# A new order of operations for each batch of a cross-attention kernel on one NeuronCore

## The chip, the core and the metric

The kernel runs on one core of a Trainium2 chip. The metric is the device time of one execution in microseconds (us): the median over several runs. A core has engines that work beside each other, each through its own instructions in order: TensorE (PE in the profile; its weight loads are listed as PEld), VectorE (DVE), ScalarE (ACT), GpSimd (POOL), and SyncE (SP), which here only issues transfers. They wait for one another at semaphores. Matmul results go to PSUM, which this kernel uses as eight banks of 512 float32 for each of 128 partitions.

## The reference

32 independent batches; `x` and `y` (in the inputs `ctx_2048`) have 256 channels by 1024 columns, float32.

```python
x_q = jnp.einsum('oc,bcn->bno', w_qk, y)
x_k = jnp.einsum('oc,bcn->bon', w_qk, x)
x_v = jnp.einsum('oc,bcn->bon', w_v, x) + b_v[None, :, None]
energy = jnp.einsum('bnc,bcm->bnm', x_q, x_k)
attention = jax.nn.softmax(energy, axis=-1)
attention = attention / (1e-07 + attention.sum(axis=1, keepdims=True))
x_r = jnp.einsum('bcn,bnm->bcm', x_v, attention)
x_r = jax.nn.relu(jnp.einsum('oc,bcn->bon', w_t, x - x_r) + b_t[None, :, None])
return x + x_r
```

Per batch there are keys from x, a 1024 by 1024 energy matrix, a softmax along its rows, a second division by its column sums, the values weighted by it, a last projection, a relu and the addition of x.

## The kernel before

**Forms.** Every operand of a matmul is kept twice: a HIGH form, the value rounded to fp32r, and a LOW form, the rest. A *product* of two 128-row operands is three matmuls, in the order of `ORDER` (line 46): high by high, high by low, low by high (left by right). So a right operand's HIGH form is read by the first and the third matmul of a product, a left operand's HIGH form by the first and the second. HIGH forms are mostly written by ACT, LOW forms by POOL or DVE, and most of them have one buffer that every batch uses again: `gf` (keys), `xf` (x), `yd` and `ysum` (y), `uf` (values).

**Chains of seven.** The keys (`k`), the projection of x (`x`) and the four pairs of energy tiles (`E0` to `E3`) are 2 by 2 block products that are made with seven products instead of eight. `chain` (line 385) names them P1 to P7. P1, P6 and P7 add to one bank, "a". Between them ACT copies that bank out (`r1`, `r2`, `r3`, into the ring `rs`), since P6 adds to what P1 left and r1 must have been read first. P2 goes to bank "b", P5 and then P3 to bank "c", P4 to bank "d" (in `k` and `x` to "a"). DVE makes the four blocks from the banks and the copies (`c11`, `c22`, `c12`, `c21`); P3 can add to bank "c" only after `c22` has read it. For a chain of keys the banks a, b, c are 2, 0, 1; of x 6, 4, 5; of energy a, b, c, d are 3, 0, 1, 2.

**Softmax.** A pair of chains E0 to E3 leaves two tiles of 128 by 1024: the even tile (n = 2p) in banks 0 and 1, the odd one (n = 2p + 1) in banks 2 and 3. For tile n: `exp` on ACT (with the row sums), `ri` (reciprocal, DVE), then for each half h `h` (HIGH form of the softmax weights in the ring `efs`, ACT), `l` (LOW form, DVE) and `sum` (their column sums in `acc`, DVE). The next pair's P1 writes bank 3, so it comes after `h`, `l` and `sum` of the odd tile's half 1; in the same way E3's tile 7 must be read out of bank 2 before kP1, and tile 6 out of bank 1 before kP5. `A` + n, c, h is the product that adds tile n's share to the output rows c, half h, in banks 4 to 7.

**Rest of a batch.** `V` + q, half: values, 12 matmuls of 256 columns each, to banks 4 to 7 before the x chain uses them; `vh`, `vl` their forms. `kc`, `kT`, `khD`, `klD`, `kTh`, `kTl`, `kh21`, `kl21`: blocks and sums of the keys and their forms in `gf`. `xh`, `xl`, `xT`, `xTh`, `xTl`: forms and sums of x in `xf`; `xTh1` is ACT's copy of the second pair of sums into the HIGH form that xP6 and xP4 read. `yh`, `yl`, `ys`, `ysh`, `ysl`: the same of y. `cols`, `inv`, `turn`: column sums, their reciprocals, and these turned (DVE). `div`, `join`, `pos`, `add`, `st`: division (DVE), addition of the projection (POOL), relu (ACT), addition of x by a transfer that POOL issues, and the store.

**What sets the order.** Each such name is a *word*: a small function that issues its instructions. Three tables of words, written out in the kernel, are the whole order: FIRST (batch 0), STEADY (run for batches 1 to 29) and LAST (the last two batches). `do` goes through a table, word by word; a plus ahead of a word means the next batch, a minus the one before. A pair (word, batch) that was done is passed over. `InOrder` (line 51) makes each engine issue in exactly the order of the words, so an instruction that waits holds up all that stands behind it on its engine, while the other engines go on. Waits between engines follow from the data: a word waits for what it reads and for the last readers of what it overwrites. All instructions pass through one helper line, L62 of the profile, so tiles tell them apart: on PE `efs,uf` is an A product, `xf,gws` the key chain, `xf,tws` the x chain, `vws,xf` the values, `gf,yd` the products 1, 2, 4 of an energy chain and `gf,ysum` its products 3, 5, 6, 7.

Of the kernel before, what the change touches and what calls it, by code (L numbers as in the profile page):

```python
# [17 lines left out]
def kernel(  # L18
# [739 lines left out]


    FIRST = """  # L760
        ys01 Sgram Scorner Swt Stp Swtc Sgh0 Ssq Sgh1 Fxh0 Sbvw Fxl0 Sgl Th22 xh1 Fxl1
        yh01 FHH0 Sgraw Sth Svh Fyh FHL0 Svl FHH1 Gh12 FLH0 FLH1 FHL1 yh00 Fraw11 ldy1
        Fkh12 Fraw22 Fkh22 Fkh11 V11 V10 ys02 yl01 ys04 ys03 ysh0 kT1 Fkl11 yl00 Fkl22 kT2
        kh21 Tl22 Fkl12 vh1 yh11 Fyl V00 Stl kT4 Sbias Th12 Gh22 kl21 FE11 kT3 vl1 FE10
        kTh0 Gl12 ysl0 Fmin1 V01 FE00 vh0 kTl0 exp1 FE01 ys11 vl0 ri1 h11 kTh1 ys12 FX11
        kTl1 Gs1 FX01 Fmin0 exp0 yh10 sum11 Gs2 l11 ri0 E1P1 Gl22 sum10 FX00 h00 h01 E1r1
        h10 E1P6 FX10 Fxw0 E1r2 sum00 ys13 ys14 l00 sum01 E1P7 l01 ysh1 l10 E1P5 yl10 E1r3
        E1c22 yl11 E1P4 +ldx0 E1c21 E1P2 Gs3 Gs4 ysl1 E1P3 A101 Fxw1 +xh0 E1c11 exp3 A110
        A001 A100 ri3 h31 E1c12 sum31 A000 l31 GhS exp2 ri2 sum21 h30 E2P1 l30 sum30 E2r1
        h21 +ldx1 A010 E2P6 sum20 E2r2 l21 E2P4 h20 +xT1 E2P7 l20 E2r3 +xT3 Ts3 E2P5 Ts1  # L770
        +xTh0 GlS +xh1 +xl0 E2c22 E2c21 E2P2 A300 exp5 E2c11 ri5 +xT2 A111 E2P3 h51 E2c12
        A310 A011 sum51 l51 h50 A301 exp4 +ldy0 Ts2 A311 E3P1 ri4 A200 sum41 sum50 Ts4
        +xl1 E3r1 +xT4 +xTl0 +ys01 +ys02 sum40 h41 +ldy1 E3P6 l41 A201 +yh01 E3r2 h40 E3P7
        E3r3 l50 l40 E3P5 +xTh1 E3c22 E3P4 E3P2 A210 E3c21 +yh00 ThS E3P3 A510 exp7 +ys04
        +xTl1 E3c11 ri7 E3c12 h70 A211 exp6 l70 sum70 A511 +ys11 +ys13 Tl12 +ys12 A501
        +ys03 ri6 +kP1 sum71 h61 l61 +kr1 A410 +kP6 sum60 +ysh0 +yl00 +yl01 +kr2 A500 +kP7
        sum61 cols +kP5 h60 +kr3 h71 l60 TlS +ys14 +kc22 +kP2 +kP3 +kc11 +kc12 +ysl0 A411
        +kP4 ++ldx0 A400 +kT1 l71 +kT3 +khD +kT2 +kT4 inv +kTh0 +kTh1 turn A711 A401 A710
        +yh10 A610 +klD +kTl1 +kh21
    """  # L780
    STEADY = """
        E0P1 E0r1 yh11 ysh1 -A700 -A701 -A611 E0P6 -div1 kTl0 -A601 kl21 -A600 E0r2 E0P7
        E0P5 -div0 E0r3 E0P4 E0c22 ysl1 yl10 E0P2 E0c21 E0c11 exp1 E0P3 yl11 +xT1 -join1
        -join0 V10 V11 ri1 h11 E0c12 V00 h10 l11 sum11 exp0 l10 ri0 sum10 vh1 E1P1 V01
        sum01 E1r1 h00 vl1 h01 vh0 +ldx1 l01 sum00 E1P6 vl0 l00 E1r2 E1P4 xP1 E1P7 +xh0
        E1r3 E1P5 E1c22 xP2 E1P2 E1c21 xr1 -pos0 E1P3 xP6 A111 xP5 exp3 E1c11 xr2 +xT2
        +xT3 +xT4 xc11 ri3 E1c12 h31 A011 xP7 A100 sum31 l31 exp2 +xl0 ri2 xr3 E2P1 sum30
        h21 h30 E2r1 sum20 A000 xP4 +xTh1 l21 E2P6 xc22 E2r2 h20 sum21 xP3 l30 E2P7 E2P5
        E2P4 xc12 l20 E2r3 E2c22 xw21 +xh1 E2c21 A101 E2P2 A110 E2P3 exp5 E2c11 ri5 E2c12
        h51 exp4 +ldy0 h50 l51 A001 sum51 A010 ri4 +xTl1 A311 A310 +ys01 h41 E3P1 A300  # L790
        E3r1 l41 sum41 E3P6 +xl1 h40 E3P5 E3r2 E3P7 +yh00 +xTh0 sum50 l50 sum40 l40 +ldy1
        E3r3 A200 E3P4 E3P2 A210 -pos1 A301 E3c22 E3c21 exp7 E3c11 ri7 h70 E3P3 A510 +yh01
        A500 A211 E3c12 +ys11 +ys03 -add1 +xTl0 +ys02 +ys04 +ys12 exp6 +yh10 A201 sum70
        l70 ri6 h61 +kP1 A410 sum71 +yl01 +ys13 +ys14 +kr1 h60 sum61 l61 +kP6 +kP5 l60
        sum60 +kr2 +kP7 +kr3 A710 +ysh0 +kP2 +kc22 h71 +kc11 +kP3 +kc12 -st1 A610 +kP4
        -add0 +yl00 +kT1 +ysl0 +kT2 +kT3 l71 +khD ++ldx0 -st0 +kT4 +kTh0 +klD +kTh1 cols
        A511 A400 +kh21 inv turn +kTl1 A501 A411 A401 A711
    """
    LAST = """
        -E0P1 -yh11 -ysh1 -kTl0 --A611 --A700 --A701 -E0r1 -E0P6 --div1 -kl21 --A601 -E0r2  # L800
        --A600 -E0P7 -E0P5 --div0 -E0r3 -E0P4 -E0c22 -E0P2 -E0P3 -E0c21 -exp1 -E0c11 -ysl1
        -ri1 -E0c12 --join1 -h11 -yl10 -yl11 -sum10 -exp0 -V11 -V10 -vh1 -l11 -sum11 -ri0
        -V00 -sum00 -h01 -E1P1 -E1r1 -V01 -vl1 -E1P6 -h00 -h10 -xP1 -l01 -sum01 -E1P5 -l00
        -l10 -vh0 -E1r2 -E1P7 --join0 -E1r3 ldx1 -vl0 -E1P4 -E1P2 -E1c22 -E1c21 -E1c11
        -xr1 xh0 -xP5 -xP2 -xP6 -E1P3 -exp3 -xc11 -A111 -ri3 xT1 -E1c12 -xr2 xT3 xT2 -h31
        -l31 -sum31 -h30 xT4 -xP7 -xr3 -xc22 -A100 -A011 -E2P1 -exp2 -E2r1 -xP3 -ri2 -l30
        -E2P6 -sum30 -xc12 -xP4 -h21 -h20 -E2r2 -E2P4 -sum21 -l21 -E2P7 xh1 -xw21 -E2P5
        xl1 -A311 -A101 -l20 -sum20 -E2r3 -E2c22 -E2P2 -E2c21 xTh0 xTh1 -exp5 -E2c11 -ri5
        -A110 -E2P3 xl0 -A001 -A000 -A010 -A301 -h51 -h50 ldy1 -E2c12 ldy0 xTl0 -l51
        -sum51 -exp4 -E3P1 -ri4 -h41 -E3r1 -A300 -E3P6 -l50 -sum41 -h40 -l41 -E3r2 yh01  # L810
        -sum50 -l40 -sum40 -E3P5 --pos0 -E3P7 -A200 -E3r3 -E3c22 -E3P2 xTl1 ys01 ys11 ys02
        --add0 --pos1 -E3P4 -A310 -A201 -E3P3 -E3c21 -A501 -A211 yh11 -exp7 -E3c11 -A500
        -A210 -ri7 -E3c12 -h70 -l70 -sum70 kP1 yh10 -exp6 -ri6 -sum71 ys12 ys14 ys13 yl10
        ys04 yl01 -h61 kr1 -A510 -h60 -l61 -sum61 kP6 -sum60 kr2 -l60 kP5 kP7 -cols -h71
        yh00 kr3 kc22 --add1 ys03 yl11 -A511 kP2 kc11 -l71 -A401 kP3 kP4 kc12 -A411 ysh0
        -A400 -A410 yl00 -A711 kh21 ysl0 kT1 khD kT2 -inv Zx1 --st1 kT4 kl21 kT3 -A710 klD
        -turn -A611 -A701 ysh1 kTh1 E0P1 -A610 -A700 E0P2 kTl1 kTh0 E0r1 -div1 E0P6 E0r2
        --st0 -A601 -A600 Zx0 kTl0 E0P7 -div0 -join0 E0r3 E0P5 E0c22 E0P4 E0c21 V00 -join1
        E0c11 exp1 E0P3 ri1 E0c12 h11 V10 V11 h10 sum11 l11 exp0 vh1 l10 sum10 E1P1 ri0
        vl1 E1r1 h00 V01 E1P6 h01 l00 E1P4 sum01 xP1 vh0 sum00 l01 E1r2 ysl1 E1P7 E1r3 xr1  # L820
        E1P5 E1P2 vl0 E1c22 -pos1 A111 E1c21 E1P3 E1c11 xP6 exp3 xr2 E1c12 xP2 ri3 h31
        A011 xc11 exp2 xP7 xr3 l31 sum31 A100 ri2 xP5 sum21 E2P1 xc22 sum30 h20 l20 E2r1
        xP4 h21 l21 E2P6 E2r2 xP3 h30 E2P7 xc12 E2P5 l30 A101 E2r3 sum20 E2c22 xw21 E2P4
        E2P2 E2c21 E2c11 E2P3 A110 exp5 A311 A001 ri5 h51 E2c12 A010 A000 exp4 l51 sum51
        E3P1 ri4 A310 h40 E3r1 h41 E3P6 sum50 l40 sum40 E3r2 h50 l41 A300 sum41 l50 E3P7
        E3P5 Zs1 E3P4 E3r3 -pos0 Zs0 E3P2 E3c22 -add1 E3c21 E3P3 exp7 A210 E3c11 E3c12
        A200 -add0 ri7 sum71 A301 A510 A211 h70 exp6 A500 A410 A201 l70 sum70 ri6 A710
        A400 sum60 sum61 A501 h71 Zn1 A511 h60 Zn0 h61 A401 l71 -st1 cols l60 inv A701
        A411 A610 l61 turn A601 Zd10 A700 -st0 A711 Zd01 Zm10 A600 Zm01 A611 Zd00 Zd11
        Za10 Zm00 Za01 Zm11 Zt10 Zt01 Za11 Za00 Zt11 Zt00  # L830
# [47 lines left out]
```

## Time and profile before

| | |
|---|---|
| median of 3 runs | 1894.0 us (1893.49 to 1894.99) |
| the profiled execution | 1892.67 us |
| its span, first to last instruction | 1890.5 us |
| granted TensorE clock, mean | 0.999 |
| PE idle before matmuls of energy, named ACT's `rs` | 9.2 us in 29 waits |
| DVE, ACT, POOL busy | 85%, 76%, 74% of the span |
| HBM | 71 GB/s over the span |

Times within a batch are counted from the span's start. The batch that is looked at closely is batch 10, from 540.75 us, where its E0P1 starts, to 599.22, where the next batch's does. A timeline row has start, busy time, engine, line, operation with output and inputs, and how many equal ones follow each other; in brackets stands the idle time just ahead of it, with the engine and tile that ended it.

### The profile page before, as it was taken

Reading aid. Unit: us, or ns where it says so; the run is one execution under the profiler, and the core shown is the slowest. Engines: PE = TensorE matmul, PEld = TensorE weight load, DVE = VectorE, ACT = ScalarE, POOL = GpSimd, SP = SyncE. Lnnn points to the kernel's source line nnn. Section 1 sums busy time; section 2 is a strip of 40 time slices with the busy share of each in tenths; the row PEclk is TensorE's granted clock in tenths of the full one; section 3 lists DMA queues with packets and bytes.
Section 4 is the critical chain, followed back from the end, with each engine's and each line's share of the span. In section 5 each row is a group of like instructions: output and inputs, shape, how many; then the busy total and the mean of one; then the engine's idle time right before and its main releaser. Section 6 shows DMA issues by size and latency. Waiting matters only on the chain. (4 is left out here: it accounts for less than half of the span.)

```text
span 1890.5 us, 25202 instructions
## 1 busy us (share of the span) xinstructions
PE 1869.4 (99%) x8680; PEld 1499.5 (79%) x8680; DVE 1609.0 (85%) x3044; ACT 1432.2 (76%) x2223; POOL 1400.0 (74%) x975
## 2 busy tenths in 40 slices
...
GB/s 96 36 81 87 45 68 87 80 79 50 74 78 79 79 56 67 79 79 78 64 60 78 79 79 77 49 76 79 83 84 45 72 85 79 79 56 68 68 90 67
DMA packets 46720, 136.76 MB, mean 72 GB/s; under 512 B 4480, under 2 KB 5376, under 8 KB 46592
## 3 DMA queue, kind: packets, MB, share of 16 engines
...
## 5 line engine op out<-in xcount | busy, mean ns | idle before, releaser
L62 PE MATMUL banks<-efs,uf 128*128 128x512 f32 x3072 | 784.3, 390 | 0.0
L62 PEld LDWEIGHTS banks<-efs,uf 128*128 128x128 f32 x3072 | 576.6, 188 | 122.8 <-DVE efs L62 0.3
L62 PE MATMUL banks<-gf,ysum 128*128 128x512 f32 x1524 | 423.2, 400 | 9.2 <-ACT rs L62 9.2
L62 ACT COPY rs<-banks 128x512 f32<-128x512 f32 (+1 forms) x475 | 279.3, 588 | 199.6 <-PE banks L62 199.1
L62 DVE SCALAR_TENSOR_TENSOR efs<-banks,small,efs 128x512 fp32r<-128x512 f32 x512 | 377.9, 744 | 40.6 <-ACT efs L62 37.0
L62 ACT ACTIVATE efs<-banks,small 128x512 fp32r<-128x512 f32 x512 | 339.4, 689 | 34.8 <-DVE small L62 22.3
L62 ACT ACTIVATE banks<-banks,small 128x1024 f32<-128x1024 f32 x256 | 278.8, 1089 | 111.9 <-DVE small L62 107.6
L62 PEld LDWEIGHTS banks<-gf,ysum 128*128 128x128 f32 x1524 | 271.0, 188 | 109.3 <-ACT rs L62 55.2
L62 DVE SCALAR_TENSOR_TENSOR acc<-banks,small,acc 128x512 f32<-128x512 f32 x448 | 329.8, 742 | 21.7 <-ACT efs L62 20.2
L62 PE MATMUL banks<-gf,yd 128*128 128x512 f32 x1158 | 319.1, 392 | 0.4 <-DVE efs L62 0.2
L62 POOL TENSOR_TENSOR xf<-sums,xf 128x1024 fp32r<-128x1024 f32 x62 | 157.6, 2543 | 189.4 <-PE banks L62 116.7
L62 POOL TENSOR_TENSOR sums<-raws 128x256 f32<-128x256 f32 (+1 forms) x188 | 173.6, 931 | 112.3 <-DMA raws<-in_ctx_dram 112.3
L62 PEld LDWEIGHTS banks<-gf,yd 128*128 128x128 f32 x1158 | 212.4, 188 | 49.9 <-POOL gf L62 5.1
L62 POOL TENSOR_TENSOR gf<-sums,gf 128x1024 fp32r<-128x1024 f32 x95 | 226.1, 2408 | 0.6 <-ACT gf L62 0.6
L62 DVE CUSTOM_DVE_ANT_0 banks<-banks,rs,small 128x512 f32<-128x512 f32 x254 | 192.7, 759 | 27.9 <-PE banks L62 11.0
L62 DVE CUSTOM_DVE_ANT_0 banks<-banks,rs 128x512 f32<-128x512 f32 x254 | 180.8, 712 | 37.7 <-PE banks L62 30.6
L62 PEld LDWEIGHTS banks<-vws,xf 128*128 128x128 f32 x1536 | 192.8, 191 | 5.4
L62 PE MATMUL banks<-vws,xf 128*128 128x256 f32 x1536 | 194.3, 283 | 0.0
L62 PE MATMUL banks<-xf,gws 128*128 128x512 f32 x651 | 189.5, 412 | 3.0 <-DVE small L62 0.2
L62 PE MATMUL banks<-xf,tws 128*128 128x512 f32 x651 | 183.0, 390 | 0.0
L62 POOL TENSOR_TENSOR ysum<-sums,ysum 128x1024 fp32r<-128x1024 f32 x64 | 154.4, 2412 | 22.2 <-ACT ysum L62 22.2
L62 POOL TENSOR_TENSOR xf<-raws,xf 128x1024 fp32r<-128x1024 f32 x62 | 149.6, 2414 | 25.5 <-ACT xf L62 25.4
...
## 6 DMA issues: line engine op xcount, KB each, us to landing
...
```

The lines of the kernel that those rows point to most:

```text
L62: self.last = getattr(self.engine, name)(*args, **kwargs)
```

## The change

Only the three tables are different. Every word is there as often as before, in another order, in FIRST, STEADY and LAST. In making the new order the HIGH form of an operand was counted as being read until the third matmul of a product. Of the difference a few lines of STEADY:

```diff
     STEADY = """
-        E0P1 E0r1 yh11 ysh1 -A700 -A701 -A611 E0P6 -div1 kTl0 -A601 kl21 -A600 E0r2 E0P7
...
+        E0P1 -A611 -turn kTh1 kh21 E0r1 kTh0 kl21 -A610 kTl1 -A700 kTl0 E0P6 E0r2 yh11
...
```

The places of which the prediction speaks follow as they stand in the built program. First PE in the second pair's chain: the rows from E2P1 to the A product behind E2P4, of a batch in the middle of the program, before.

```order
L62 MATMUL banks<-gf,yd 128x512 x3
L62 MATMUL banks<-efs,uf 128x512 x3
L62 MATMUL banks<-xf,tws 128x512 x3
L62 MATMUL banks<-gf,ysum 128x512 x3
L62 MATMUL banks<-xf,tws 128x512 x3
L62 MATMUL banks<-gf,ysum 128x512 x6
L62 MATMUL banks<-gf,yd 128x512 x3
L62 MATMUL banks<-efs,uf 128x512 x3
```

They are E2P1, A000, xP4, E2P6, xP3, then E2P7 with E2P5, E2P4 and A101. The same place on PE in the change:

```order
L62 MATMUL banks<-gf,yd 128x512 x3
L62 MATMUL banks<-xf,tws 128x512 x6
L62 MATMUL banks<-gf,ysum 128x512 x3
L62 MATMUL banks<-efs,uf 128x512 x3
L62 MATMUL banks<-gf,ysum 128x512 x6
L62 MATMUL banks<-gf,yd 128x512 x3
L62 MATMUL banks<-efs,uf 128x512 x3
```

These are E2P1, xP4 with xP3, E2P6, A311, then E2P5 with E2P7, E2P4 and A000: the last two products of the x chain are both ahead of E2P6, and two products instead of one stand between E2P6 and E2P7.

ACT beside it, from h21 to xw21: the copies into `rs` are the readings E2r1, E2r2 and E2r3, and the CAST into `xf` from `sums` is xTh1. Before:

```order
L62 ACTIVATE efs<-banks,small 128x512 x2
L62 COPY rs<-banks 128x512
L62 CAST xf<-sums 128x1024
L62 COPY rs<-banks 128x512
L62 ACTIVATE efs<-banks,small 128x512
L62 COPY rs<-banks 128x512
L62 ACTIVATE xe<-banks,xbias 128x512
```

In the change, on ACT, from the same h21, where the two ACTIVATE into `efs` are h30 and h20 and the CAST from `raws` is xh1:

```order
L62 ACTIVATE efs<-banks,small 128x512
L62 COPY rs<-banks 128x512
L62 ACTIVATE efs<-banks,small 128x512 x2
L62 COPY rs<-banks 128x512
L62 CAST xf<-raws 128x1024
L62 COPY rs<-banks 128x512
L62 ACTIVATE xe<-banks,xbias 128x512
```

xTh1 has gone from between E2r1 and E2r2 (it now stands behind E3r2), and xh1 has come between E2r2 and E2r3.

Last, PE from E3P1 into the next batch's keys, before:

```order
L62 MATMUL banks<-gf,yd 128x512 x3
L62 MATMUL banks<-efs,uf 128x512 x3
L62 MATMUL banks<-gf,ysum 128x512 x9
L62 MATMUL banks<-efs,uf 128x512 x3
L62 MATMUL banks<-gf,yd 128x512 x6
L62 MATMUL banks<-efs,uf 128x512 x6
L62 MATMUL banks<-gf,ysum 128x512 x3
L62 MATMUL banks<-efs,uf 128x512 x12
L62 MATMUL banks<-xf,gws 128x512 x3
L62 MATMUL banks<-efs,uf 128x512 x3
L62 MATMUL banks<-xf,gws 128x512 x9
L62 MATMUL banks<-efs,uf 128x512 x3
```

That is E3P1, A300, E3P6 with E3P5 and E3P7, A200, E3P4 with E3P2, A210 with A301, E3P3, four A products, kP1, A410, kP6 with kP5 and kP7, and A710. The same stretch of PE in the change:

```order
L62 MATMUL banks<-gf,yd 128x512 x3
L62 MATMUL banks<-efs,uf 128x512 x6
L62 MATMUL banks<-gf,ysum 128x512 x9
L62 MATMUL banks<-gf,yd 128x512 x3
L62 MATMUL banks<-efs,uf 128x512 x6
L62 MATMUL banks<-gf,yd 128x512 x3
L62 MATMUL banks<-gf,ysum 128x512 x3
L62 MATMUL banks<-efs,uf 128x512 x12
L62 MATMUL banks<-xf,gws 128x512 x3
L62 MATMUL banks<-efs,uf 128x512 x6
L62 MATMUL banks<-xf,gws 128x512 x12
L62 MATMUL banks<-efs,uf 128x512 x3
```

Now E3P1 is followed by A310 and A301 ahead of E3P6, and kP1 by A510 and A501 ahead of kP6; kP6, kP5, kP7 and kP2 follow each other, with A401 ahead of kP3. From E3P7 to kP1 there are nine products (before, ten).

The order of the other words of a batch, with its neighbours, is changed in the same way; the x rows of the batch after next are loaded as `ldx1` at a batch's end and `ldx0` in its second pair, where before it was the other way round. In FIRST, PE's FHH0 and FHL0 (first keys) stand ahead of Ssq (the product of two weight matrices) instead of behind it.

More of the change, by code (lines that the diff above doesn't have):

```diff
@@ L760 @@
     FIRST = """
[L761 to L778, printed above, removed]
@@ new lines @@
+        FX11 E1P6 h01 Gs1 yl10 h00 E1r2 FX00 kTl0 E1P7 +ldx0 l00 l01 l10 Fxw1 sum00 E1r3
+        E1P5 E1P4 +xh0 E1c22 Gs2 E1c21 E1P2 Fxw0 E1P3 A100 Gl12 Gs4 Ts1 yl11 exp3 E1c11
+        Gs3 Ts3 ri3 E1c12 h31 ysl1 Ts2 exp2 A110 l31 sum31 A101 +ldx1 A010 A111 +xl0 GhS
+        ri2 E2P1 h21 A001 E2r1 sum30 sum21 l21 h20 E2P6 +xT3 Ts4 +xT1 l20 +ldy0 E2P5 E2r2
+        h30 sum20 l30 E2P7 E2P2 E2P4 E2r3 A011 +xh1 E2c22 E2P3 +xT2 A301 GlS A000 A201
+        A300 E2c21 A311 E2c11 exp5 ri5 E2c12 h51 l51 sum51 exp4 +yh01 ri4 E3P1 sum50 h41
@@ new lines @@
+        E3r1 h40 +xT4 h50 A211 E3P6 E3r2 l41 sum41 l40 l50 E3P5 E3P7 +xTh1 E3r3 E3P4 sum40
+        E3P2 A310 E3c22 E3c21 E3P3 +xTh0 +xl1 +ys01 +ys02 +yl01 A210 +ys04 +xTl1 exp7
+        +yh00 E3c11 A511 ri7 +ldy1 E3c12 h70 exp6 l70 sum70 ri6 A510 A200 A501 ThS h61
+        +kP1 sum71 A410 l61 +kr1 sum61 +kP6 +xTl0 h60 +ys03 +kr2 +ysh0 TlS +kP5 sum60 +kP7
+        A401 l60 +kP2 +ys11 +kr3 +yl00 cols +kc22 +kP3 A411 A500 +kc11 +kc12 +ys12 h71
+        +ysl0 +kP4 +ys14 A400 +khD +yh10 +kT1 +ys13 l71 +kT2 A701 +klD +kT4 inv +kT3 A710
@@ L787 @@
[L787 to L797, printed above, removed]
+        E0P1 -A611 -turn kTh1 kh21 E0r1 kTh0 kl21 -A610 kTl1 -A700 kTl0 E0P6 E0r2 yh11
```

89 lines of the change are left out of this document (53 added, 36 removed).

## The prediction

> **What bounds the kernel now.** I read the page's first part, then the weight loads' waits, then one batch on TensorE row by row.
>
> ```profile
> span 1890.5 us, 25202 instructions
> PE 1869.4 (99%) x8680; PEld 1499.5 (79%) x8680; DVE 1609.0 (85%) x3044; ACT 1432.2 (76%) x2223; POOL 1400.0 (74%) x975
> ```
>
> TensorE (PE) is named busy for 99%, yet a matmul's shown time overlaps the next one's, so a short stall hides in it. Starts are what count. This is PE's timeline in batch 10; columns are start, busy time, operation with its tiles, count, and idle time before.
>
> ```profile
> 545.52 1.55 PE L62 MATMUL banks<-gf,ysum 128*128 128x512 f32 x6
> ...
> 548.97 4.48 PE L62 MATMUL banks<-vws,xf 128*128 128x256 f32 x36
> 553.28 0.86 PE L62 MATMUL banks<-gf,yd 128*128 128x512 f32 x3
> ...
> 567.10 0.85 PE L62 MATMUL banks<-gf,ysum 128*128 128x512 f32 x3
> 567.79 0.84 PE L62 MATMUL banks<-xf,tws 128*128 128x512 f32 x3
> 568.94 1.65 PE L62 MATMUL banks<-gf,ysum 128*128 128x512 f32 x6 [0.31 <-ACT rs L62]
> 570.43 0.84 PE L62 MATMUL banks<-gf,yd 128*128 128x512 f32 x3
> ...
> 573.83 2.88 PE L62 MATMUL banks<-efs,uf 128*128 128x512 f32 x12
> 576.55 0.84 PE L62 MATMUL banks<-gf,yd 128*128 128x512 f32 x3
> 577.23 0.84 PE L62 MATMUL banks<-efs,uf 128*128 128x512 f32 x3
> 578.07 2.60 PE L62 MATMUL banks<-gf,ysum 128*128 128x512 f32 x9
> 580.51 0.85 PE L62 MATMUL banks<-efs,uf 128*128 128x512 f32 x3
> ```
>
> Twelve wide matmuls start in 576.55 - 573.83 = 2.72 us, 0.227 each, so a product of three is 0.68; a narrow one is (553.28 - 548.97) / 36 = 0.120. A batch has six chains of 7 products and 32 A products, 74 x 3 = 222 wide matmuls, and 4 x 12 = 48 narrow ones; they need 222 x 0.227 + 48 x 0.120 = 56.2 us. The next rows are a whole batch by windows (window, length, busy time of PE and of the weight loads, and so on) and the waits of the weight loads over the span (us, times, longest).
>
> ```profile
> 540.75:599.22 58.47, 58.08 (x272) 46.63 (x270) 50.13 (x95) 44.67 (x69) 43.81 (x32) 1.00 0.27 72
> ...
> PEld banks L62 <- ACT rs L62: 76.4, 191, 1.0
> PEld banks L62 <- DVE sums L62: 15.7, 30, 0.5
> PEld banks L62 <- DVE efs L62: 10.8, 33, 0.4
> ```
>
> A batch takes 58.47 us (540.75 is E0P1's start, 599.22 the next one's), so 2.3 us are stalls. No other engine is over 50.13. The loads of the same batch say where:
>
> ```profile
> 568.94 1.23 PEld L62 LDWEIGHTS banks<-gf,ysum 128*128 128x128 f32 x6 [0.73 <-ACT rs L62]
> ...
> 578.07 1.23 PEld L62 LDWEIGHTS banks<-gf,ysum 128*128 128x128 f32 x6 [0.42 <-ACT rs L62]
> 579.71 0.53 PEld L62 LDWEIGHTS banks<-gf,ysum 128*128 128x128 f32 x3 [0.41 <-ACT rs L62]
> ...
> 588.84 0.53 PEld L62 LDWEIGHTS banks<-xf,gws 128*128 128x128 f32 x3 [0.42 <-ACT rs L62]
> 589.71 0.53 PEld L62 LDWEIGHTS banks<-xf,gws 128*128 128x128 f32 x3 [0.33 <-DVE efs L62]
> 590.50 0.53 PEld L62 LDWEIGHTS banks<-xf,gws 128*128 128x128 f32 x3 [0.26 <-ACT rs L62]
> ...
> 592.93 0.54 PEld L62 LDWEIGHTS banks<-xf,gws 128*128 128x128 f32 x3 [0.52 <-DVE sums L62]
> ```
>
> In order they are E2P7, E3P6, E3P7, kP6, kP5, kP7 and kP3. A load runs ahead of its matmul, so a wait costs less than it shows: at E2P7 nine matmuls from 567.79 took 2.64 instead of 2.04 us, 0.60 lost for a wait of 0.73; from 577.23 twelve took 3.28 instead of 2.72, 0.56 for 0.42 + 0.41. I take wait minus 0.15: 0.58, 0.27, 0.26, 0.27, 0.18, 0.11, 0.37, together **2.04 us a batch**. That is what an order can win.
>
> **Why they wait.** Bank a is written by a product, read by ACT, and added to by the next product.
>
> ```profile
> 567.35 1.05 ACT L62 CAST xf<-sums 128x1024 fp32r<-128x1024 f32 x1 [0.46 <-PE banks L62]
> ...
> 568.31 0.57 ACT L62 COPY rs<-banks 128x512 f32<-128x512 f32 x1
> ...
> 577.43 0.59 ACT L62 COPY rs<-banks 128x512 f32<-128x512 f32 x1 [0.18 <-PE banks L62]
> ```
>
> E3P1 starts at 576.55, its reading at 577.43 (0.88 later), E3P6 at 578.07: 1.52 us from product to product with a free ACT. One product between covers 2 x 0.68 = 1.36, and 0.16 plus a slow second matmul is lost; two between cover 2.04, with 0.52 to spare. E2P7 is worse: ACT stands first in xTh1 (567.35), which waits 0.46 us for xP4, the last reader of the high form that it overwrites; E2r2 starts only at 568.31, where E2P6 at 567.10 would have let it start at 567.98.
>
> **The change, part by part.** No instruction is added or removed; all terms are stalls per batch, and the new table runs for 29 batches.
>
> *E2P7.* Two products now stand between E2P6 and E2P7 (A311 and E2P5), and on ACT xTh1 is gone from before E2r2; behind E2r2 is xh1, whose readers xP2 and xP3 are ahead of E2P6. E2r2 follows h30 and h20, which need nothing from E2P6. Gone: **0.58**, at worst 0.27 stays if these two run late.
>
> *E3P6 and kP6.* Each has two products before it (A310 and A301; A510 and A501). Ahead of E3r1 ACT now has exp4, yh00 and h41; they use the spare 0.52 at the worst. Gone: 0.27 + 0.27 = **0.54**.
>
> *kP5* waits for l61, the last reader of its bank. On DVE l61 gets sum60 ahead of it (0.66 us, the step from 574.72 to 575.38 in the DVE rows below), and on PE kP5 gets one product more ahead of it (0.68) but loses kP6's stall as cover. Gone: **0.10**, between nothing and 0.18.
>
> *Kept.* E3P6 to E3P7 and kP6 to kP7 still have one product between: 0.26 stays, and kP7, which hid behind kP5's wait, rises from 0.11 to 0.26: **-0.15**. kP7 to kP3 still has two: 0.37 stays.
>
> *New waits.* From a pair's last bank-a product to the next pair's first, the chain runs through reading, blocks with minima, exponential, reciprocal and weights. In E2 before (ACT and DVE of the timeline):
>
> ```profile
> 569.94 0.59 ACT L62 COPY rs<-banks 128x512 f32<-128x512 f32 x1 [0.46 <-PE banks L62]
> ...
> 570.74 0.70 DVE L62 CUSTOM_DVE_ANT_0 banks<-banks,rs 128x512 f32<-128x512 f32 x1 [0.48 <-PE banks L62]
> ...
> 571.64 0.76 DVE L62 CUSTOM_DVE_ANT_0 banks<-banks,rs,small 128x512 f32<-128x512 f32 x1
> ...
> 572.50 1.09 ACT L62 ACTIVATE banks<-banks,small 128x1024 f32<-128x1024 f32 x1 [0.44 <-DVE small L62]
> ...
> 573.74 0.16 DVE L62 RECIPROCAL small<-small 128x1 f32<-128x1 f32 x1 [0.31 <-ACT banks L62]
> ...
> 574.03 0.76 DVE L62 CUSTOM_DVE_ANT_0 banks<-banks,rs,small 128x512 f32<-128x512 f32 x1
> ...
> 574.72 0.75 DVE L62 SCALAR_TENSOR_TENSOR efs<-banks,small,efs 128x512 fp32r<-128x512 f32 x1
> 575.38 0.74 DVE L62 SCALAR_TENSOR_TENSOR acc<-banks,small,acc 128x512 f32<-128x512 f32 x1
> ```
>
> E2P7 starts at 568.94, the last reader of E3P1's bank ends at 576.12: 7.18 us, and E3P1 came at 576.55, 0.43 later. In the new order nine products stand between E2P7 and E3P1 and nine between E3P7 and kP1: 10 x 0.68 = 6.8 us. The chain's steps hold some 0.35 us in which it waited for PE itself: 0.12 at the first reading (1.00 against the 0.88 above), and, at the first block, for E2P5, which now is ahead of E2P7:
>
> ```profile
> 580.81 0.58 ACT L62 COPY rs<-banks 128x512 f32<-128x512 f32 x1
> ...
> 581.43 0.70 DVE L62 CUSTOM_DVE_ANT_0 banks<-banks,rs 128x512 f32<-128x512 f32 x1
> ```
>
> That is E3's first block, 0.62 after its reading against 0.80. Another 0.05 is the second block, which waited for E2P4. So the chain needs between 6.83 and 7.18 us for 6.8: E3P1 and kP1 wait between nothing and 0.38 each, and up to 0.1 more in the second matmul. The rows show most of those waits ended by PE, so I lean to the lower end: 0.2 each, **-0.40**. For E1P1 the cover is four products and 36 narrow matmuls, 4 x 0.68 + 36 x 0.120 = 7.04, and for E2P1 eleven products, 7.5: nothing, at worst 0.1.
>
> A wide matmul's pitch of 0.227 sets these covers. The Trainium skill, page "TensorE: Matmul & The Clock Gate", section "Back-to-back issue gap", gives about 216 ns for 512 columns. By it ten products would cover 6.5 us instead of 6.8 and each new wait would be 0.3 us longer, an estimate from that page of 0.6 us a batch less won, about 1891; this trace does not agree, and its 0.227 decides.
>
> *First and last batches.* The first batch's FHH0 and FHL0 now stand before Ssq, where PE idled:
>
> ```profile
> 7.06 1.99 PE L62 MATMUL banks<-z 128*128 128x256 f32 x8 [0.57 <-ACT z L62]
> ```
>
> That is 0.57 us. The rest of FIRST and LAST I cost at nothing, as both have chains with one and with two products between in both versions; the bound is one batch's 2.04 us either way.
>
> **The sum.** 0.58 + 0.54 + 0.10 - 0.15 - 0.40 = 0.67 us a batch; 29 x 0.67 = 19.4, with 0.57 about 20 us. The profiled execution took 1892.7 (span 1890.5), so this gives 1872.7 for it; the median of the runs is 1894.0, 1.3 more: **1874 us**.
>
> **Rivals.** *More is won.* If no new wait appears, 29 x 1.07 + 0.6 = 32 us: 1862; with kP7 as small as now and kP5's wait wholly gone 29 x 1.30 + 0.6 = 38: 1856. For it: the stretches of the chain that waited for PE. Against: 6.83 leaves nothing spare in 6.8.
>
> *The softmax chain becomes the bound (the other side).* Place: from E0P7, E2P7 and E3P7 to the next pair's first product. If the chain needs 7.2 us in the new order too, E1P1 waits 0.16, E3P1 and kP1 0.4 each, with 0.1 for each second matmul 1.2 in all: the 1.07 won is gone, about 1896. From there each tenth costs 0.3 us a batch. If it needs what lay between those products before, 568.94 to 576.55 and, for E0P7 to E1P1, 545.52 to 553.28 (7.76), the waits are 0.7 + 0.3 + 0.95 + 0.95 and 0.4 for second matmuls, 3.3 against 1.07: 29 x 2.2 = 64 us more, 1958. For it: E2's 7.18 is a measured need. Against: in these rows the softmax weights were ready 0.4 us before the product came.
>
> *The waits move to POOL.* klD must end before E0P1's second matmul.
>
> ```profile
> 596.86 4.79 POOL L62 TENSOR_TENSOR gf<-sums,gf 128x1024 fp32r<-128x1024 f32 x2
> ```
>
> The first of these two is klD, ending near 599.26, for a matmul at 599.22 + 0.23: 0.2 to spare. In the new order kT2 and klD still end POOL's queue of the batch. Each tenth more than those 0.2 costs 2.9 us; with half a microsecond late E0P1 waits 0.3 29 x 0.3 = 9 us: 1883, inside the range.
>
> *The change does not do what it says*, that is, ACT still waits for high forms being read: then E2P7's 0.58 stays, 29 x 0.58 = 17 us: 1891.
>
> **Chances.** My forecast (1864 to 1884) 0.55; more won (1855 to 1864) 0.13; the chain, POOL or ACT gives back part, 1884 to 1890, 0.13; all of it, 1890 to 1898, 0.10; slower 0.09, most of it the chain. A measurement of this kernel tells about 0.2% (3.8 us) from no change. Faster 0.81, same 0.10, slower 0.09. Low end: 38 us won, 1856. High end: both new waits at 0.48 and E1P1's at 0.1 leave 1.07 - 1.06, nothing, and the first batch's 0.6: 1893; the range is 1856 to 1893.
>
> **What would show it.** Right: E0P1 to E0P1 falls to about 57.8 us; E2P6, E3P1 and kP1 are each followed about 2.04 us later by the next product of their chain on bank a; the loads' waits on ACT's rs fall from 76.4 to below 40 us; waits at E3P7, kP7 and kP3 stay. Wrong: waits of over 0.6 us at E3P1 or kP1 on DVE, at xP3 on DVE's xe, or at E0P1 on POOL's gf; or a first batch that is later by several microseconds.

## The result, and the profile after

| | before | after |
|---|---|---|
| median | 1893.74 us (1893.36 to 1894.99) | 1876.94 us (1876.58 to 1877.14) |
| the profiled execution | 1892.67 us | 1876.58 us |
| its span | 1890.5 us | 1874.5 us |
| granted TensorE clock | 0.999 | 0.999 |

The changed kernel takes 0.991 of the time before (95% interval 0.9893 to 0.9927): 16.8 us less, where 20 were forecast.

The page's first part of the changed kernel shows nothing of it; busy shares hardly moved.

```profile
span 1874.5 us, 25084 instructions
PE 1861.9 (99%) x8680; PEld 1506.3 (80%) x8680; DVE 1596.7 (85%) x3044; ACT 1439.3 (77%) x2223; POOL 1407.3 (75%) x975
```

Starts show it. These are the rows of PE's timeline with E0P1 of batch 1 and of batch 30, the ends of the 29 batches that STEADY orders; first the kernel before, then the change (start, busy time, operation).

```profile
72.45 1.24 PE L62 MATMUL banks<-gf,yd 128*128 128x512 f32 x3
...
1768.86 0.86 PE L62 MATMUL banks<-gf,yd 128*128 128x512 f32 x3
```

```profile
71.89 0.85 PE L62 MATMUL banks<-gf,yd 128*128 128x512 f32 x3
...
1754.40 0.84 PE L62 MATMUL banks<-gf,yd 128*128 128x512 f32 x3
```

The 29 batches took 1696.41 us and now 1682.51: 13.9 less, 0.48 a batch. (The batches are numbered from 0 here and in the experiments; the "tenth batch" of the rows is batch 9, which stands in the kernel before from E0P1's row at 540.68 to the next one's at 599.17.) The first batch is 72.45 - 71.89 = 0.56 shorter. The last part is (1890.5 - 1768.86) - (1874.5 - 1754.40) = 1.54 shorter. Together 16.0, the whole difference of the spans.

Where a batch still stalls is told by the weight loads. First their waits over the whole span (us, times, longest), then, from their timeline, the loads of the tenth batch, 535.89 to 593.82, that waited longest (in brackets the wait and what ended it).

```profile
PEld banks L62 <- ACT rs L62: 28.2, 68, 0.4
PEld banks L62 <- DVE sums L62: 16.5, 31, 0.9
PEld banks L62 <- ACT banks L62: 14.9, 35, 0.5
PEld banks L62 <- issue: 11.5, 31, 0.8
PEld banks L62 <- POOL gf L62: 9.5, 50, 0.2
```

```profile
564.27 0.53 PEld L62 LDWEIGHTS banks<-gf,yd 128*128 128x128 f32 x3 [0.23 <-DVE efs L62]
...
570.62 0.53 PEld L62 LDWEIGHTS banks<-gf,yd 128*128 128x128 f32 x3 [0.36 <-issue]
...
574.34 0.53 PEld L62 LDWEIGHTS banks<-gf,ysum 128*128 128x128 f32 x3 [0.42 <-ACT rs L62]
...
581.47 0.53 PEld L62 LDWEIGHTS banks<-xf,gws 128*128 128x128 f32 x3 [0.42 <-ACT banks L62]
...
585.15 1.22 PEld L62 LDWEIGHTS banks<-xf,gws 128*128 128x128 f32 x6 [0.41 <-ACT rs L62]
...
587.58 1.22 PEld L62 LDWEIGHTS banks<-xf,gws 128*128 128x128 f32 x6 [0.52 <-DVE sums L62]
```

In order they are E2P4, E3P1, E3P7, kP1, kP7 and kP3. E2P7, E3P6, kP6 and kP5 are no longer among them; E3P1 and kP1 are new. The waits on ACT's `rs` (over the whole span) fell from 76.4 to 28.2 us; those on "ACT banks" and "issue" are nearly all kP1's and E3P1's. Neither name is of what held them: both start a constant 0.15 us behind DVE's last reading of their bank.

This is E2's stretch of PE and ACT in that batch.

```profile
561.59 0.84 PE L62 MATMUL banks<-gf,ysum 128*128 128x512 f32 x3
562.27 0.84 PE L62 MATMUL banks<-efs,uf 128*128 128x512 f32 x3
562.95 1.52 PE L62 MATMUL banks<-gf,ysum 128*128 128x512 f32 x6
...
570.65 0.94 PE L62 MATMUL banks<-gf,yd 128*128 128x512 f32 x3
```

```profile
560.42 0.59 ACT L62 COPY rs<-banks 128x512 f32<-128x512 f32 x1
560.90 1.27 ACT L62 ACTIVATE efs<-banks,small 128x512 fp32r<-128x512 f32 x2
562.47 0.59 ACT L62 COPY rs<-banks 128x512 f32<-128x512 f32 x1 [0.29 <-PE banks L62]
562.95 1.05 ACT L62 CAST xf<-raws 128x1024 fp32r<-128x1024 f32 x1
```

E2P6 starts at 561.59, its reading 0.88 later at 562.47, with ACT waiting for it; E2P7, the second half of the six from 562.95, at 563.63, 2.04 after E2P6 and without a stall. E3P1 comes 7.02 us after E2P7, where it had been 7.61. That ACT no longer stands at a high form that is still being read is shown by a row of its waits that the changed kernel does not have. Before:

```profile
ACT xf L62 <- PE banks L62: 23.7, 58, 0.7
```

### The profile page after: what moved, and what is told of

The parts are those of the page before. It is cut to its first block, busy times and chain, and to the rows that moved or that the text cites. A ratio compares the mean times of both kernels' runs of the same rounds, so it can differ in the third digit from the quotient of the medians.

```text
span 1874.5 us, 25084 instructions
## 1 busy us (share of the span) xinstructions
PE 1861.9 (99%) x8680; PEld 1506.3 (80%) x8680; DVE 1596.7 (85%) x3044; ACT 1439.3 (77%) x2223; POOL 1407.3 (75%) x975
## 4 chain that ended last, share of the span: by engine, by line
PE 94%; DVE 2%; ACT 1%; issue 1%; POOL 1%; DMA 0%; DVEq 0%; ACTq 0%
PE banks L62 94%; DVE sums L62 1%; ACT rs L62 1%; POOL xf L62 0%; DVE banks L62 0%; POOL sums L62 0%; ACT banks L62 0%; DVE acc L62 0%; DVE efs L62 0%; DMA z<-in_L_xattn_w_qk_dram 0%; POOL raws L62 0%; ACT efs L62 0%; POOL z L62 0%; POOL yd L62 0%; DMA out_dram<-z 0%
## 5 line engine op out<-in xcount | busy, mean ns | idle before, releaser
L62 PE MATMUL banks<-efs,uf 128*128 128x512 f32 x3072 | 771.7, 390 | 0.0
L62 PE MATMUL banks<-gf,ysum 128*128 128x512 f32 x1524 | 415.1, 394 | 0.0
L62 DVE SCALAR_TENSOR_TENSOR acc<-banks,small,acc 128x512 f32<-128x512 f32 x448 | 325.1, 743 | 17.5 <-ACT efs L62 15.2
L62 PEld LDWEIGHTS banks<-gf,ysum 128*128 128x128 f32 x1524 | 276.7, 188 | 72.2 <-ACT rs L62 14.9
L62 PE MATMUL banks<-gf,yd 128*128 128x512 f32 x1158 | 330.4, 397 | 0.5 <-DVE acc L62 0.2
L62 POOL TENSOR_TENSOR sums<-raws 128x256 f32<-128x256 f32 (+1 forms) x188 | 190.1, 1064 | 116.7 <-DMA raws<-in_ctx_dram 116.6
L62 POOL TENSOR_TENSOR xf<-sums,xf 128x1024 fp32r<-128x1024 f32 x62 | 147.9, 2408 | 97.6 <-ACT xf L62 97.5
L62 POOL TENSOR_TENSOR z<-z,xe 128x1024 f32<-128x1024 f32 x62 | 149.1, 2405 | 61.8 <-DVE z L62 61.8
L62 PE MATMUL banks<-xf,gws 128*128 128x512 f32 x651 | 179.6, 407 | 4.1 <-DVE sums L62 0.4
L62 PE MATMUL banks<-xf,tws 128*128 128x512 f32 x651 | 173.3, 390 | 0.0
```

The lines of the kernel that those rows point to most:

```text
L62: self.last = getattr(self.engine, name)(*args, **kwargs)
```

## The experiments

Two pictures were to be told apart. **Sum:** each stall counts for itself, so that one taken away is won in full. **Loop:** PE and the softmax chain go round from one pair's first product to the next pair's (P1, P6, P7, reading, blocks, exponential, reciprocal, weights, P1), and a stall taken away inside a turn is worth only what the next P1 has to spare. In the kernel before, P1 comes 0.44 us after its bank's last reader at E3P1 and kP1, 0.33 at E2P1, 0.72 at E1P1. Where E3P1 or kP1 itself waits, it comes 0.15 after that reader; this time is called the handoff below, and the spare is what lies above it. A *turn* is the time from one P1's start to the next P1's; lengths of turns and late starts below are means of batches 3 to 27, and "0.24 and 0.08 late" is said of a product's first matmul and of its second.

The kernel before was run again beside each group of experiments (1892.06, 1891.34 and 1891.42 us, against 1893.74 in the result); the changed kernel was not. So an experiment that starts from the changed kernel is compared with it by their traces: there a turn that the edit leaves alone agrees to 0.02 us with the changed kernel's. The edits are shown as pieces of STEADY, cut at both ends.

**Two products ahead of E2P7**, in the kernel before:

```diff
-  h20 sum21 xP3 l30 E2P7 E2P5 E2P4 xc12
+  h20 sum21 xP3 l30 E2P5 E2P7 E2P4 xc12
```

> Theory (local cover): in the kernel before, only E2P5 goes ahead of E2P7, so two products stand between E2P6 and E2P7 while ACT still has xTh1 ahead of E2r2. E2r2 starts at the same time, 1.21 us after E2P6, and ends before the two products do, so E2P7 loses nothing; the 0.43 us to spare ahead of E3P1 take up that it starts 0.2 us later. Won: 0.56 to 0.60 us a batch, about 16 us, near 1878, as much as the whole change. Rival (a loop of latencies): E2P7 is later, so E3P1 is later, and the stall only moves there: under 0.2 us a batch, 1888 or more.

Measured: 1884.56 us beside 1892.06, 0.9961 (0.9946 to 0.9976), 7.5 us or 0.26 a batch. That lies between the theory's 0.56 to 0.60 a batch and the rival's 0.2, so neither number came true. E2P7's stall of 0.59 went, as the starts of its matmuls show; the loads of a batch show what came:

```profile
574.00 0.53 PEld L62 LDWEIGHTS banks<-gf,yd 128*128 128x128 f32 x3 [0.44 <-ACT banks L62]
```

That is E3P1, which did not wait before; its two first matmuls start 0.24 and 0.08 late. E2's turn (E2P1 to E3P1) fell from 11.52 to 11.17 us, 0.35, nearer to the 0.28 that E3P1 had to spare than to the 0.59 of the stall; the other 0.07 is the chain itself, whose last reader `sum51` starts 10.28 us after E2P1 in place of 10.36. Of the 0.35, E3's turn gave 0.07 back. The loop is the nearer picture.

**xTh1 behind E2r2**, alone and together with the edit above:

```diff
-  sum20 A000 xP4 +xTh1 l21 E2P6 xc22 E2r2 h20
+  sum20 A000 xP4 l21 E2P6 xc22 E2r2 +xTh1 h20
```

> In the kernel before, only xTh1 goes behind E2r2 on ACT; PE's order stays, one product between E2P6 and E2P7. Theory (the wait for the high form's last reader delays E2r2): E2r2 starts 0.88 after E2P6 instead of 1.21, the loads' wait at E2P7 falls from 0.73 to about 0.42, 0.3 us a batch, 9 us, near 1885. Rival (one product of cover is what costs, the form's wait is hidden): no change, 1893 to 1895.

> Both edits in the kernel before. Theory: the second product hides E2r2 whether xTh1 is ahead of it or not, so this is the same as the two products alone within 3 us, near 1878; the two gains do not add. Rival (each has its own cost): the gains add, 1869.

Measured: 1887.00 us alone, 0.9973 (0.9963 to 0.9984), 5.1 us won where the theory had 9; 1888.11 with both, 0.9979 (0.997 to 0.9989), 4.0 us won, which neither the theory (1878) nor the rival (1869) had. The first two rows are loads of the kernel with the copy moved alone, the third of the one with both.

```profile
567.21 1.24 PEld L62 LDWEIGHTS banks<-gf,ysum 128*128 128x128 f32 x6 [0.42 <-ACT rs L62]
...
574.89 0.53 PEld L62 LDWEIGHTS banks<-gf,yd 128*128 128x128 f32 x3 [0.28 <-ACT banks L62]
```

```profile
575.22 0.53 PEld L62 LDWEIGHTS banks<-gf,yd 128*128 128x128 f32 x3 [0.62 <-ACT banks L62]
```

With the copy gone from its place, E2P7 keeps 0.16 + 0.11, the price of a single product between, and E3P1 begins to wait. So of E2P7's 0.59 the copy was 0.32 and the missing product 0.27. Both edits together win less than either. In both kernels h20 now stands behind xTh1 (it starts 4.37 us after E2P1 in place of 3.74), l20 comes later with it, and so does the chain's first block E2c22, which is behind l20 on DVE (5.75 and 5.76, against 5.62 with the two products alone). So E2P7 comes 3.57 us after E2P1 with the copy moved alone and 4.11 with both, and yet E3P1 comes at nearly the same time, 11.27 and 11.30: with both edits it waits 0.40 + 0.08. Most of what was taken from E2P7's wait was handed to the next P1.

**xTh1 back ahead of E2r2**, in the changed kernel, twice: alone, and with what it reads.

```diff
-  E2P6 h30 h20 E2r2 -add1 +xT1 A311
+  E2P6 h30 h20 +xTh1 E2r2 -add1 +xT1 A311
...
-  E3P7 E3P4 A300 A210 +xTh1 +ys02
+  E3P7 E3P4 A300 A210 +ys02
```

```diff
-  E2P6 h30 h20 E2r2 -add1 +xT1 A311 +xh1 +xT2
...
+  E2P6 h30 h20 -add1 +xT1 +xT2 +xT4 +xTh1 E2r2 A311 +xh1
```

> In the changed kernel, only xTh1 goes back between the weights h20 and E2r2 on ACT; its last readers xP4 and xP6 are done by then, so it waits for no reader. Theory (an operation of 1.05 us ahead of a reading that has 0.5 us to spare): E2P7 waits about 0.5 us and loses 0.1 more in its second matmul, 17 us more, 1892 to 1896. Rival (only the wait for the form's reader matters, not the place of the copy): no change from 1877.

> The changed kernel with the high form xTh1, and the add and the transposes xT1, xT2 and xT4 that it reads, moved ahead of E2r2, so that the copy stands in ACT's queue ahead of E2r2 as in the kernel before, but waits for no matmul there. Theory: its 0.5 to 0.6 us on ACT delays E2r2 and with it E2P7 and the softmax chain by 0.1 to 0.2 us a batch: 1878 to 1883. Rival: the copy's place in ACT's queue carries the whole of the stall that went: E2P7's 0.45 + 0.11 come back in full, 16 us, 1893.

Alone it took 2076.05 us, 1.0975 (1.0957 to 1.0993), far from both the theory and the rival. This run says nothing of the copy's place: xTh1 stands ahead of xT2 and xT4 there, so the high form is taken from what the ring's place held before, and the low form from the difference. But it shows how late sums on POOL reach PE. PE, POOL, ACT, and two windows (window, length, busy times, after them the granted clock):

```profile
625.82 1.55 PE L62 MATMUL banks<-efs,uf 128*128 128x512 f32 x6
631.91 4.21 PE L62 MATMUL banks<-gf,ysum 128*128 128x512 f32 x9 [4.55 <-ACT rs L62]
635.92 1.35 PE L62 MATMUL banks<-gf,yd 128*128 128x512 f32 x3
```

```profile
621.36 4.76 POOL L62 TENSOR_TENSOR xf<-raws,xf 128x1024 fp32r<-128x1024 f32 x2
```

```profile
630.39 0.40 ACT L62 CAST yd<-raws 128x256 fp32r<-128x256 f32 x1 [5.26 <-DMA raws<-in_ctx_dram]
...
631.29 0.58 ACT L62 COPY rs<-banks 128x512 f32<-128x512 f32 x1
```

```profile
629.00:634.00 5.00, 2.09 (x5) 1.70 (x6) 2.58 (x4) 2.46 (x5) 3.48 (x3) 0.62 0.06 23
634.00:640.00 6.00, 6.00 (x21) 4.78 (x21) 3.00 (x9) 3.44 (x6) 2.01 (x2) 0.75 0.00 0
```

POOL's sums start only at 617.47, right behind the copy's end (617.34), and its low forms of x (xl0, xl1), behind the sums, ended at 626.12; the load of y into the place of `raws` that xl1 had read landed 4.3 us behind that, ACT waited 5.26 us for it at yh00, and E3r1 stands behind yh00 in ACT's queue, so E3P6 waited 4.55. Then nine matmuls took 635.92 - 631.91 = 4.01 us, 0.446 each in place of 0.227; the windows' granted clocks of 0.62 and 0.75 are means over the time before, at and behind a clock of 0.50.

With its sums moved along, the kernel took 1880.34 us, 0.994 (0.9925 to 0.9956), as its theory had it (1878 to 1883). ACT and the loads of that run:

```profile
562.95 1.06 ACT L62 CAST xf<-sums 128x1024 fp32r<-128x1024 f32 x1
563.89 0.60 ACT L62 COPY rs<-banks 128x512 f32<-128x512 f32 x1
```

```profile
564.54 0.53 PEld L62 LDWEIGHTS banks<-gf,ysum 128*128 128x128 f32 x3 [0.29 <-ACT rs L62]
...
571.67 0.53 PEld L62 LDWEIGHTS banks<-gf,yd 128*128 128x128 f32 x3 [0.44 <-issue]
```

The copy waits for nothing here and still delays E2r2; with two products as cover E2P7 loses 0.13 in place of 0.59, E3P1 0.08 more than in the changed kernel, and the 29 batches 3.6 us. So the removed wait for the high form and the second product were what counted; the copy's mere place on ACT, with the sums' on POOL, is worth 3.6 us of 14.

**Third products earlier**, in the changed kernel, so that the last block (`c12`) comes sooner: in E2, in E3 (there with sum70 ahead of l70), in both, and in both with E3P4 ahead of E3P7.

```diff
-  E2P2 A101 E2P3 A110 +xT3 E2c11 exp5 ri5 A211 A010 A001 h51 E2c12 sum51
+  E2P2 E2P3 A101 A110 +xT3 E2c11 E2c12 exp5 ri5 A211 A010 A001 h51 sum51
...
-  E3P7 E3P4 A300 A210 +xTh1
+  E3P7 E3P4 A300 +xTh1
...
-  E3c11 A511 -add0 +ys04 +ys11 exp7 A200 A411 A201 ri7 E3c12 h70 l70 exp6 sum70
+  E3c11 E3c12 A210 A511 -add0 +ys04 +ys11 exp7 A200 A411 A201 ri7 h70 sum70 l70 exp6
```

(The first hunk is the edit in E2, the other two are the one in E3, where A210 is moved behind E3P3 so that E3P3 comes one product sooner; the fourth kernel has E3P4 and E3P7 exchanged as well.)

> In the changed kernel E2P3 goes ahead of A101, and on DVE E2c12 directly behind E2c11, where DVE idled for E2P3; so the reciprocal and sum51, l51 behind it come about 0.7 us earlier. Theory (E3P1 waits for l51 because E2c12 stands between the reciprocal and the weights): E3P1's wait of 0.21 us a batch goes, 6 us, near 1871. Rival (the wait moves on to the next chain, or the exponential of the even tile is late): no change, 1875 to 1878.

> The same in the fourth pair: E3P2 and E3P3 go ahead of A210, E3c12 directly behind E3c11, and sum70 ahead of l70. Theory: kP1's wait of 0.27 us a batch goes; POOL's klD, which has 0.2 us to spare ahead of E0P1, holds back at most 0.1 of it: 5 to 8 us, 1869 to 1872. Rival (POOL's queue from xTh1 to klD is the bound of this stretch): the wait moves to E0P1, 1875 to 1878.

> Both edits. Theory: the gains add, 11 to 14 us, 1863 to 1866. Rival (klD binds): as one of them alone, 1870 or more.

> Both edits, and E3P4 goes ahead of E3P7, so that two products stand between E3P6 and E3P7. Theory (local cover): the 0.27 us a batch lost at E3P7 go, but E3P7 starts 0.41 us later, and kP1's chain has about 0.4 to spare after the earlier E3P3: 4 to 8 us less than with both edits, 1857 to 1861. Rival (a loop of latencies): the wait moves to kP1 or, through xTh1 and POOL, to E0P1: no change or up to 4 us more than with both edits.

Measured, beside 1891.34 us: 1882.47 (0.9954, 0.9939 to 0.9968), 1882.33 (0.9952, 0.9937 to 0.9967), 1888.69 (0.9986, 0.9976 to 0.9995) and 1900.33 (1.0047, 1.0032 to 1.0062). All are slower than the changed kernel; the theories had all four faster, and no rival came out as it stood. Between E0P1 of batch 1 and of batch 30 they take 5.6, 5.6, 11.7 and 23.4 us more. DVE, then the loads, of the run with E2P3 early:

```profile
569.78 0.76 DVE L62 CUSTOM_DVE_ANT_0 banks<-banks,rs,small 128x512 f32<-128x512 f32 x1
...
570.46 0.16 DVE L62 RECIPROCAL small<-small 128x1 f32<-128x1 f32 x1
571.44 0.75 DVE L62 SCALAR_TENSOR_TENSOR acc<-banks,small,acc 128x512 f32<-128x512 f32 x1 [0.83 <-ACT efs L62]
```

```profile
572.97 0.53 PEld L62 LDWEIGHTS banks<-gf,yd 128*128 128x128 f32 x3 [0.54 <-issue]
```

The early c12 (569.78) now stands ahead of the reciprocal, which starts 32.43 us after the batch's E0P1 (538.03), against 568.12 - 535.89 = 32.23 in the changed kernel. From there h51, sum51, l51 and E3P1 are each 0.2 late, and 0.2 x 29 is about the 5.6 us. In the changed order c12 fills the time in which sum51 waits for h51, and costs nothing. E3 repeats it at kP1, and the two add, since they lie in different turns. Taking away E3P7's stall on top only moved it: E3P3 (0.27 + 0.11) and kP1 (0.68 + 0.08) wait instead.

**One product between E3P1 and E3P6**, in the changed kernel, as there was before:

```diff
-  E3P1 A310 A301 +xl0
+  E3P1 A310 +xl0
...
-  E3P7 E3P4 A300 A210
+  E3P7 E3P4 A301 A300 A210
```

> The changed kernel with one product (A301) taken from between E3P1 and E3P6 and put behind E3P4, so that one product stands there as in the kernel before. Theory of the loop: E3P6 waits 0.16 + 0.11 again, and kP1's 0.19 + 0.08 goes, since kP1 is released by the same chain at the same time with one product's place filled differently: no change, within 2 us of the changed kernel. Rival (each wait counts for itself, as the forecast summed them): 29 x 0.27 = 8 us slower, about 1885.

Measured: 1876.89 us, 0.9922 (0.9907 to 0.9938), as the loop's forecast had it. By the ratios it is 2 us behind the changed kernel; but those go by two measurements of the kernel before that differ by 2.3 us, and in the traces its 29 batches take 1682.8 us against 1682.5, where the rival had 8 more. Its loads in the tenth batch:

```profile
570.88 0.53 PEld L62 LDWEIGHTS banks<-gf,yd 128*128 128x128 f32 x3 [0.36 <-issue]
...
572.51 0.53 PEld L62 LDWEIGHTS banks<-gf,ysum 128*128 128x128 f32 x3 [0.42 <-ACT rs L62]
...
573.47 0.53 PEld L62 LDWEIGHTS banks<-gf,ysum 128*128 128x128 f32 x3 [0.42 <-DVE efs L62]
...
581.71 0.53 PEld L62 LDWEIGHTS banks<-xf,gws 128*128 128x128 f32 x3 [0.18 <-ACT banks L62]
```

E3P6 waits again (572.51), and kP1 (581.71) hardly; E3P5 (573.47) took over E3P7's wait. The 0.27 of E3P6 came back, kP1's 0.27 went, and the batches' time did not change, as the loop has it and the sum does not. The second product between E3P1 and E3P6 is worth nothing here.

**The key part alone**, in the kernel before, and with E2P5 ahead of E2P7:

```diff
-  E0P1 E0r1 yh11 ysh1 -A700 -A701 -A611 E0P6
+  E0P1 E0r1 yh11 ysh1 -A700 -A611 E0P6
...
-  h60 sum61 l61 +kP6 +kP5
+  h60 sum61 l61 A511 +kP6 +kP5
...
-  +kTh1 cols A511 A400 +kh21 inv turn +kTl1 A501 A411 A401 A711
+  +kTh1 cols A400 +kh21 inv turn +kTl1 A501 A411 A401 A711 A701
```

(A701 is moved in FIRST as well.)

> The kernel before, with the key part alone rearranged as in the change: one product (A511) taken from behind kP4 and put ahead of kP6, so that two stand between kP1 and kP6, and one product (A701) taken from the front of the batch (between E0P1 and E0P6) to the end of the batch before it. Theory (softmax chain as a loop from one first product P1 to the next; a removed stall is worth only what the next first product has to spare): kP6's 0.27 us and kP5's 0.17 a batch go, kP7's rises by about 0.06 to 0.15, and E1P1, which had 0.72 us to spare ahead of it, gives up the 0.68 of the product that left: 0.2 to 0.3 us a batch, 6 to 9 us, so 1884 to 1887 beside a kernel before of 1892 to 1893. Rival: E0P1 then waits for the keys' last copy (klD) or kP1's chain, the batch is as long as before: 1891 to 1894.

> The run above with E2P5 moved ahead of E2P7 as well. Theory: the two places are different turns of the loop, so their gains add: 0.26 (measured for the two products alone) and 0.2 to 0.3, 14 to 16 us in all, 1876 to 1879: the whole gain of the change from three moved products, without its rearrangement of E3. Rival (the gain hangs on E3's products or on the copies that were moved): 1882 to 1886.

Measured: 1901.65 us beside 1891.42, 1.0053 (1.0035 to 1.0071), slower; with E2P5 moved 1894.83, 1.0018 (1.0008 to 1.0028). Both forecasts missed, and both rivals with them: the theory had 1884 to 1887 and 1876 to 1879. The first kernel's waits over the span, the loads at the front of the tenth batch and POOL there:

```profile
PEld banks L62 <- POOL gf L62: 30.5, 85, 0.5
```

```profile
545.82 0.30 PEld L62 LDWEIGHTS banks<-gf,ysum 128*128 128x128 f32 x2 [0.45 <-POOL gf L62]
...
548.18 1.01 PEld L62 LDWEIGHTS banks<-gf,ysum 128*128 128x128 f32 x5 [0.44 <-POOL gf L62]
```

```profile
541.00 7.13 POOL L62 TENSOR_TENSOR gf<-sums,gf 128x1024 fp32r<-128x1024 f32 x3
```

POOL makes the keys' three low forms klD, kTl1 and kTl0 one behind another, 541.00 to 548.13. E0P6's second matmul is released when the second of them ends (545.82 is close to 541.00 + 2/3 of 7.13 = 545.75), E0P7's when the third does (548.18, 548.13). With A701 gone from ahead of them both come up to 0.68 us early and wait: 0.30 each, 0.6 of the 0.68. The turn from kP1 to E0P1 gained what the loop says: one product longer, 0.68, but only from 11.86 to 12.26; the turn from E0P1 fell by just 0.07, 12.55 to 12.48. E1P1 had time to spare (the changed kernel uses it up), and another queue had none. The second kernel is 6.8 us faster than the first, beside the 7.5 of E2P5 alone: gains in different turns add, and of that forecast only this part held.

The changed kernel has the same kind of product move, and does not pay this: it still has three products ahead of E0P6 and two between E0P6 and E0P7 (there E0P4 and E0P2), and the one that left came from behind E0P7. Its turn from E0P1 fell by 0.64 of the product's 0.68, 12.55 to 11.91, and the one from kP1 grew by 0.52, 11.86 to 12.38.

No run beat the changed kernel; the one with a single product between E3P1 and E3P6 equals it.

## Why the prediction came out as it did

Its direction and its range held; the point, 1874, was 2.9 us low, hardly more than the 2.4 us by which the kernel before differed between measurements. The signs that it named came too: the batch fell to 57.99 us (57.8 forecast), E2P7, E3P6 and kP6 come 2.04, 2.15 and 2.14 us after the product before them on their bank, and the waits on `rs` are below 40. The places of the stalls were right, and the misses are in the sizes of small terms, some of which cancel. Each stall is measured from the starts of matmuls, the first of a product and its second, as a mean over the batches:

| step | forecast, us a batch | measured |
|---|---|---|
| E2P7 gone | 0.58 | 0.59 |
| E3P6 and kP6 gone | 0.54 | 0.54 |
| kP5 less | 0.10 | 0.17, all of it |
| kP7 more | -0.15 | -0.17 |
| E3P7 and kP3 | kept | kept (0.27, 0.38) |
| E3P1 waits | -0.20 | -0.21 |
| kP1 waits | -0.20 | -0.27 |
| E1P1, E2P4, E0P7 | nothing | -0.19 |
| sum | 0.67 | 0.46; by the batches' length 0.48 |

(The 0.02 between the last two is in starts late by under 0.04 us and in small shifts of the kept stalls, which are not counted.)

*E2P7, E3P6, kP6.* Right in place and size. The doubt that the two products might run late did not come true.

*The new waits.* "The chain needs between 6.83 and 7.18 us for 6.8" was the step that the sign hung on. In the tenth batch E3P1's bank is free of its last reader, l51, 6.87 us after E2P7's start:

```profile
568.12 0.16 DVE L62 RECIPROCAL small<-small 128x1 f32<-128x1 f32 x1 [0.62 <-ACT banks L62]
568.24 0.76 DVE L62 CUSTOM_DVE_ANT_0 banks<-banks,rs,small 128x512 f32<-128x512 f32 x1
...
569.10 0.75 DVE L62 SCALAR_TENSOR_TENSOR acc<-banks,small,acc 128x512 f32<-128x512 f32 x1
569.76 0.74 DVE L62 SCALAR_TENSOR_TENSOR efs<-banks,small,efs 128x512 fp32r<-128x512 f32 x1
```

569.76 + 0.74 = 570.50, from 563.63. It lies at the low end, as the forecast leaned; E3P1 starts 0.15 later. That 0.15 from DVE's end to PE's start was not in the working, and it is most of the wait. At kP1 the chain is longer: its last reader `sum70` ends 7.01 us after E3P7 starts (a mean), and that is why kP1 waits more than the 0.20 of the forecast.

*What was mis-sized.* E1P1 was put at "nothing, at worst 0.1", and E2P4 and E0P7 are not in the sum at all. They lose 0.07 (E1P1), 0.07 (E2P4, which waits for DVE's l30) and 0.05 (E0P7, for POOL's low form), 0.19 a batch or 5.5 us. That is the step that failed, with kP1's 0.07. Going the other way, LAST, costed at nothing, gave 1.54 us, which no run takes apart, and kP5 0.07 a batch. The first batch's 0.57 measured 0.56, in part by luck: 0.54 of it is there once the first keys are made (the next product starts at 18.12 in place of 18.66), and the rest of FIRST, not counted, is 0.37 us further ahead by kP1 (59.94 against 60.85) and has lost nearly all of that by the next E0P1.

*The reasoning under it.* The working took stalls as terms that add, less new waits at E3P1 and kP1. The runs show this to hold only turn by turn. By turns the batch's 0.49 (means of batches 3 to 27) is: E0P1 to E1P1 0.64 less, E1 0.01 less, E2 0.39 less, E3 0.03 more, the keys 0.52 more. E2 gave its spare at E3P1 (0.28), and its chain ends 0.11 sooner; E3 gave nothing, as kP1's new wait took E3P6's 0.27; from the keys and E0 together came 0.12. "2.04 us a batch. That is what an order can win" was therefore no measure of what can be won: a stall inside a turn is partly the wait for a chain that needs its time anyway.

*The rivals.* More won: no, the new waits came. The chain as the bound: at 6.87 and 7.01 and not 7.2, so it took 0.48 and not 1.2; the runs with the third products early show the price of each 0.2 more, 5.6 us, as forecast ("each tenth costs 0.3 us a batch" for three joins, 0.1 for each). Waits on POOL: klD cost nothing, but the key part alone showed kTl1 and kTl0, behind it in the same queue, a few tenths from deciding. That ACT would still wait at a high form: its row is gone.

*What stays open.* That the order of E2 brings most of the gain is shown by its turn and by the runs that move E2P5 and xTh1. What the new order of the keys and of E0 is worth by itself in the changed kernel was not run; the 0.12 is read from the two turns alone.
